# Two graph layers on one core: due times of their own for the first two batches, and head outputs transposed over 97 rows

## The chip, the core and the metric

The kernel runs on one core of one Trainium2 chip. The core has five engines with instruction queues of their own: TensorE (PE; its weight loads are shown apart as PEld), VectorE (DVE), ScalarE (ACT), GpSimd (POOL) and SyncE (SP), which only starts transfers here. Each engine works through its queue in order; engines wait for one another through semaphores. The metric is the time of one execution on the device in microseconds (us); lower is better.

## The reference

Two layers run on `x` of shape (16, 1024, 256), with a 0/1 adjacency matrix `adj` of shape (16, 1024, 1024) of type int32.

```python
# layer 0: attention with 8 heads of 32 columns, masked by adj
e = einsum('whqd,whkd->whqk', q, k)            # q, k, v = heads(x @ Wq), ...
e = where(e >= 0, e, 0.2 * e)
attn = softmax(where(adj > 0, e, NEG), axis=-1)
h = einsum('whqk,whkd->whqd', attn, v)         # -> (w, n, 256)
out = layernorm(h) ; out = concat([out, x]) @ Wffn.T
x1 = layernorm(out) + x
# layer 1: two graph attentions, a norm, a feed-forward, a norm
h = gat(gat(x1, adj, W1, a1), adj, W2, a2)     # softmax of leaky(Wh1 + Wh2^T), masked, axis=1; @ Wh
h = layernorm(x1 + h)
y = layernorm(h + relu(h @ w_ff1 + b_ff1) @ w_ff2 + b_ff2)
```

Each of the 16 batches is independent of the others.

## The kernel before

Everything runs on one core, batch after batch, but the stages of neighbouring batches overlap. A stage is a Python generator, a thread. It yields requests: `take` and `give` for buffers of a pool, `wait` and `fire` for events, `on(PE=..., DVE=...)` for an engine with an estimated cost, and `start` for another thread with an **aim**, a due time. The class `Order` (L34) runs all threads against a plan clock while the kernel is built and emits their instructions. Among the operations that could start within 300 ns of the earliest one, it emits the one with the smallest aim (L150 and what follows). So an aim is a rank: it decides the order on each engine's queue and the order in which waiting threads get buffers, but no engine waits for an aim to pass, except that the scores of a batch may not be planned more than `lead` ahead of theirs (L570). The order is fixed when the program is built; on the chip only semaphores act.

The aims are shares of `SLOT` = 253 us of plan time. They stand in the dictionary `AIM` (L254 to 258). Those of the projections of batch b (`project`, L513) count from the planned start of batch b - 1's scores (`begin`); for batch 0 they count from -253 us. Those of a batch's later stages (`rest`, L968) count from the moment when its last head is planned.

The stages of a batch are these.

- `project`: `x_pair` (L430) loads and transposes x; `qk_part` (L446) makes q and k, splits them in two parts and stores them to DRAM; `load_stacks` (L523) reads them back on SP, head by head; `v_part` (L483) makes v; `make_mask` (L419) starts eight `mask_part` threads (sixteen half ones for batch 0), each of which loads adjacency rows on ACT's queue (L393), turns them to fp8 on DVE (L399), transposes them on PE (L409) and copies them to the mask on ACT (L413). There are two masks; the one of batch b + 2 can be begun when batch b has given its own back, which is after its second graph attention.
- `all_scores` (L558) and `weights` (L585): for each of 8 heads and 8 tiles of 128 keys, scores on PE (L578), scaling on ACT (L596) or, in batch 0, on DVE too (L594), a maximum on DVE (L598), an exponential on ACT (L601) and the product with the mask on POOL (L605). Their aims advance with `pace(b)` (L555): a slot of 253 us, times `fast0` for batch 0 and `fast1` for batch 1. There are five buffers `p` for these tiles.
- `all_values` (L608): the product of the weights with v on PE (L627). v carries a column of minus ones, so 33 columns per head hold the output and its sum. The two halves of the 1024 queries stand one below the other in PSUM, at partitions 0 to 32 and 64 to 96.
- `after_head` (L637): the head's output is copied to SBUF (`ho`), transposed by four PE transposes (L653), and divided by its sums on DVE (L658, L660).
- `rest`: `rows_pair` (L702, layer 0's norms and output), the first graph attention (`attention`, L825, with `attend` on DVE at L814, L817, L820 and the scaling on ACT at L822), `second_rows` (its product, L851), the second graph attention, `normed_pair` (its product, L876), and `feed_forward` (L930; L916 and L944 on PE).

Of the kernel before, what the change touches and what calls it, by code (L numbers as in the profile page):

```python
# [20 lines left out]
P = 128  # L21
# [164 lines left out]
def wait(event):  # L186
    return "wait", event
# [6 lines left out]
def take(pool):  # L194
    return "take", pool
# [6 lines left out]
def start(thread, aim):  # L202
    return "start", (thread, aim)
# [21 lines left out]
def unshifted_path(  # L225
# [8 lines left out]
    nc = tc.nc  # L234
    B, N, D = x.shape
# [15 lines left out]
    PACE = SLOT / (H * NT // 2)  # L251


    AIM = dict(mask0=0.6, x=0.818, x_step=0, mask=0.747, mask_step=0.0264, qk0=0.614, qk1=0.898, qk_step=0.0231, v0=0.832,  # L254
               v1=0.974, v_step=0.0591, rows=-0.244, rows_step=0.0408, first0=0.12, first1=0.252,
               graph0=-0.009, graph1=0.21, graph_step=0, second=0.355, second_step=0.0335, normed=0.78,
               normed_step=0.026, ff_wait=(None, 0, 1, 0), ff=(0.532, -0.011, 0.487, 0.497), ff_step=0.0386,
               fast0=0.4, fast1=0.85, fast15=0.832, lead=3.15)

    const = ctx.enter_context(tc.tile_pool(name="const", bufs=1))  # L260
    sb = ctx.enter_context(tc.tile_pool(name="sb", bufs=1))
# [3 lines left out]
    bufs = dict(misc=3, scores=2, acc=1, p=5, stacks=2, stage=2, adj=2, adjb=2, pair=18,  # L265
                xT=2, v=2, mask=2, hn=1, w8=2, big=1, job=1)
    work = Order(**bufs)

    def misc(dtype=FT):
        return psum.tile([P, HALF], dtype, tag="misc", name="ps_m", bufs=bufs["misc"])  # L270
# [148 lines left out]
    def make_mask(b, t0):  # L419
        yield take("mask")  # L420
        masks[b] = buf([P, NT * N], "mask", "mask", F8)
        parts = [(t, (kh,)) for kh in range(NH) for t in range(NT)] if b == 0 else [(t, (0, 1)) for t in range(NT)]
        for n, (t, halves) in enumerate(parts):
            yield start(mask_part(b, t, halves), t0 + (AIM["mask" if b else "mask0"] + AIM["mask_step"] * n) * SLOT)

    def mask_of(b, t):

# [49 lines left out]
    def project_qk(b, g, t0):  # L477
        scratch[b, g] = dram.tile([2, P, 2, N], FT, name="qk_halves")
        for o in range(2):
            for nh in range(NH):  # L480
                yield start(qk_part(b, g, o, nh), t0 + (2 * o + nh) * AIM["qk_step"] * SLOT)

    def v_part(b, g, u):  # L483
        yield wait(("xT", b, u))
# [18 lines left out]
    def project_v(b, g, t0):  # L503
        yield take("v")
        v = buf([P, NT, G * VW + 31], "v", "v")
        vs[b, g] = v
        yield on(POOL=500)
        nc.gpsimd.memset(v[:, :, G * VW:], 0.0)
        nc.gpsimd.memset(v[:, :, :G * VW].rearrange("p t (h c) -> p t h c", c=VW)[:, :, :, DH:], -1.0)
        for u in range(NP):  # L510
            yield start(v_part(b, g, u), t0 + AIM["v_step"] * u * SLOT)

    def project(b, t0):  # L513
        yield take("xT")
        xTs[b] = buf([P, DC, N], "xT", "xT")
        for u in range(NP):
            yield start(x_pair(b, u), t0 + (AIM["x"] + AIM["x_step"] * u if b else 0.0) * SLOT)
        yield start(make_mask(b, t0), t0 + (0.5 if b else 0.0) * SLOT)
        for g in range(H // G):
            yield start(project_qk(b, g, t0 + AIM[("qk0", "qk1")[g]] * SLOT), t0)  # L520
            yield start(project_v(b, g, t0 + AIM[("v0", "v1")[g]] * SLOT), t0 + (0.8, 1.0)[g] * SLOT)

    def load_stacks():  # L523

# [112 lines left out]
    def after_head(b, h, acc):  # L637
        if h == 0:
            yield take("hn")
            hn[b] = buf([P, NT, D], "hn", "hn")  # L640
            checks[b] = small.tile([P, NSUM + NSCORE], FT, name="check", bufs=2)
            yield fire(("hn open", b))
        yield wait(("hn open", b))
        yield take("pair")
        ho = buf([P, HALF], "pair", "ho")
        engine = yield evacuate(HALF)
        copy(engine, ho, acc)
        yield give("acc")
        yield take("misc")
        pt = misc()  # L650
        yield on(PE=450)
        for i in range(TPH):
            nc.tensor.transpose(pt[:, i * P:(i + 1) * P], ho[:, i * P:(i + 1) * P], ident)  # L653
        yield give("pair")
        src = pt.rearrange("p (i j c) -> p j i c", i=TPH, j=NH)
        rd = checks[b][:, h * NT:(h + 1) * NT].rearrange("p (j i) -> p j i", j=NH)
        yield on(DVE=210)
        nc.vector.reciprocal(rd, src[:, :, :, DH])  # L658
        yield on(DVE=430)
        nc.vector.tensor_tensor(hn[b].rearrange("p (j i) d -> p j i d", j=NH)[:, :, :, h * DH:(h + 1) * DH],  # L660
                                src[:, :, :, :DH], rd[:, :, :, None].to_broadcast([P, NH, TPH, DH]), op=OP.mult)
        yield give("misc")
        yield fire(("hn", b, h))
# [161 lines left out]
    def attention(b, s, rows, at):  # L825

        yield take("w8")
        firsts[b, s] = buf([P, 2, N], "w8", "first")
        for nh in range(NH):
            yield start(first_half(b, s, nh), at(AIM[("first0", "first1")[s]]))  # L830
        for t in range(NT):
            yield wait(("row", b, s, t))
        second = small.tile([P, NT], FT, name="second", bufs=2)
        yield on(ACT=220)
        nc.scalar.activation(second, scores_of(b, s)[:, :, 1], AF.Exp, scale=1.0 - ALPHA)
        sums = small.tile([P, NT], FT, name="sums", bufs=2)
        yield take("big")
        big = buf([P, NT, N], "big", "att")
        yield fire(("graph", b, s))
        for j in range(NT):  # L840
            yield start(attend(b, s, big, rows, j, second, sums), at(AIM[("graph0", "graph1")[s]] + AIM["graph_step"] * j))
        for j in range(NT):
            yield wait(("att", b, s, j))
        yield give("w8")
        return big
# [19 lines left out]
    def normed_pair(b, u, big, y2):  # L865

        tiles = (2 * u, 2 * u + 1)
        yield wait(("x1", b, u))
        x1 = x1s.pop((b, u))
        yield take("misc")  # L870
        pa = misc()
        for i, t in enumerate(tiles):
            for half in range(2):
                yield on(PE=1720)
                for j in range(half * NT // 2, (half + 1) * NT // 2):
                    nc.tensor.matmul(pa[:, i * D:(i + 1) * D], big[:, j, t * P:(t + 1) * P], y2[:, j, :D],  # L876
                                     start=(j == 0), stop=False)
            yield on(PE=430)
            as_rows(pa, i, x1, i)
        yield fire(("weighed", b, u))  # L880
        yield give("pair")
        y, rows, srcs = yield from taken_out(pa, "y")
        mv, rs = yield from stats(srcs)
        yield from normalized(rows, srcs, mv, rs)
        yield take("pair")
        rT = buf([P, DC, 2 * P], "pair", "rT")
        yield take("misc")
        pt = misc()
        yield on(PE=450)
        transposes(pt, rows)  # L890
        yield give("pair")
        for dc in range(DC):
            yield from by_columns(rT[:, dc, :], pt[:, dc * 2 * P:(dc + 1) * 2 * P], k["gl1c"][:, dc:dc + 1],
                                  k["bl1c"][:, dc:dc + 1])
        yield give("misc")

        if b + 1 < B and AIM["ff_wait"][u] is not None:
            yield wait(("graph", b + 1, AIM["ff_wait"][u]))
        yield start(feed_forward(b, u, rT), work.now + (AIM["ff"][u] if b + 1 < B else 0.04 * u) * SLOT)

    def as_rows(pa, i, srcT, t):

# [25 lines left out]
        yield fire(done + (hp,))  # L928

    def feed_forward(b, u, rT):  # L930
        due = work.now + (AIM["ff"][u] if b + 1 < B else 0.04 * u) * SLOT
        yield take("job")
        hid = {}
        for hp in range(HC // 2):
            yield start(hidden(hid, rT, hp, ("hid", b, u)), due + AIM["ff_step"] * hp * SLOT)
        for hp in range(HC // 2):
            yield wait(("hid", b, u, hp))
        yield take("misc")
# [29 lines left out]
    def rest(b):  # L968
# [3 lines left out]
        def at(share):  # L972
            return t0 + share * SLOT
# [6 lines left out]
        for q in range(NH):  # L980
            yield start(head_stats(b, q), at(0))
        for u in range(NP):
            yield start(rows_pair(b, u), at(AIM["rows"] + AIM["rows_step"] * u))
        for u in range(NP):
            yield wait(("hn used", b, u))
        yield give("hn")
# [2 lines left out]
        yield take("w8")  # L989
        y2 = buf([P, NT, YW], "w8", "y2")  # L990
        for i in range(NT):
            yield start(second_rows(b, big, y1, y2, i), at(AIM["second"] + AIM["second_step"] * i))
        for i in range(NT):
            yield wait(("row", b, 1, i))
        yield give("big")
        yield give("w8")
        for u in range(2):
            yield start(fetch_x1(b, u), at(AIM["normed"]))
        big = yield from attention(b, 1, y2, at)
        yield give("mask")  # L1000
        yield start(count(b), at(1.0))
        for u in range(NP):
            yield start(normed_pair(b, u, big, y2), at(AIM["normed"] + AIM["normed_step"] * u))
        for u in range(NP):
            yield wait(("weighed", b, u))
            if u + 2 < NP:
                yield start(fetch_x1(b, u + 2), at(AIM["normed"]))
        yield give("big")
        yield give("w8")

# [409 lines left out]
```

## Time and profile before

| | |
|---|---|
| median of 3 runs | 4531.88 us (4531.49 to 4532.59) |
| the profiled execution | time 4533.91 us, span 4532.1 us, granted clock 0.985 |
| PE busy | 4352.1 us (96%), 20299 matmuls |
| DVE busy | 3338.5 us (74%) |
| ACT busy | 2888.7 us (64%) |
| POOL busy | 2469.0 us (54%) |
| L653, the transposes of the heads' outputs | 512 of 128x128, 80.1 us |
| L605, POOL's product with the mask | 1024, 2228.3 us |

The span runs from the first instruction to the last. An engine's busy time is the time in which at least one of its instructions ran. Ends of matmuls are modelled and their runs overlap, so the distance between starts says more about PE than the length of one. A line such as L653 is a line of the kernel. "Idle before" is the time for which an engine had nothing to do, and behind it stands what ended it.

### The profile page before, as it was taken

The page shows a single profiled execution, that of the slowest core. Times are in us where ns is not written, and L with a number is a line of the kernel's source. Part 1 is how long each engine was busy: PE and PEld are TensorE (multiplying, and loading weights), DVE is VectorE, ACT ScalarE, POOL GpSimd, SP SyncE. Part 2 cuts the span into 40 slices and gives each one's busy share as a digit, 9 for nine tenths or more (in the row PEclk, how much of TensorE's full clock was granted, in tenths as well). Part 3 has the DMA queues.
Part 4 walks back from the last instruction along what each step waited for, and adds up shares of the span by engine and source line. Part 5 has one row for each costly group of instructions (what it writes and reads, how often), then busy time and mean ns, then how long its engine had stood idle before and what let it go on. Part 6 is the DMA issues. An engine that isn't in the chain of part 4 may idle for free.

```text
span 4532.1 us, 57096 instructions
## 1 busy us (share of the span) xinstructions
PE 4352.1 (96%) x20299; PEld 2889.7 (64%) x20299; DVE 3338.5 (74%) x5265; ACT 2888.7 (64%) x4012; POOL 2469.0 (54%) x1544
## 2 busy tenths in 40 slices
PE   7888999999999999999999999999999999999998
PEld 3354756666666676666767666676666667666587
DVE  6876678877787777768777777787768777776754
ACT  5656565566666666676666666666666676666631
POOL 4856465455565545655565565556655564565610
PEclk8989999999999999999999999999999999999999
DMA  6422223132232312323132232322323232232100
GB/s 181 116 65 68 73 61 96 54 84 76 62 98 63 105 56 76 94 59 110 57 88 73 59 100 70 101 66 72 85 66 100 63 93 62 69 92 54 26 22 20
DMA packets 156208, 343.57 MB, mean 76 GB/s; under 512 B 21750, under 2 KB 24332, under 8 KB 155916
## 3 DMA queue, kind: packets, MB, share of 16 engines
q1 hardware_dynamic: 109836, 255.93, 20.2%
q10 hardware_dynamic: 46080, 83.91, 6.2%
q8 instruction: 164, 2.69, 0.3%
q14 instruction: 128, 1.05, 0.1%
HBM read 239.09 MB, written 100.66 MB: 75 GB/s over the span
## 4 chain that ended last, share of the span: by engine, by line
PE 68%; DVE 19%; POOL 5%; issue 4%; ACT 3%; DMA 0%; SPq 0%; ACTq 0%; POOLq 0%; DVEq 0%
PE ps_a L627 15%; PE ps_s L578 9%; PE ps_m L876 8%; PE ps_m L851 7%; PE ps_m L916 7%; PE ps_m L944 6%; DVE att L817 5%; DVE att L814 5%; POOL p L605 4%; DVE p L598 4%; PE ps_m L461 3%; PE ps_m L761 2%; PE ps_m L729 2%; PE ps_m L732 2%; PE ps_m L347 2%
## 5 line engine op out<-in xcount | busy, mean ns | idle before, releaser
L605 POOL TENSOR_TENSOR p<-p,mask 128x1024 f32<-128x1024 f32 x1024 | 2228.3, 2193 | 1588.5 <-ACT p L601 1492.6
L598 DVE TENSOR_TENSOR p<-p,ps_s 128x1024 f32<-128x1024 f32 x1024 | 1210.8, 1213 | 407.9 <-ACT p L596 406.4
L601 ACT ACTIVATE p<-p 128x1024 f32<-128x1024 f32 x1024 | 1081.4, 1058 | 385.8 <-DVE p L598 363.3
L596 ACT ACTIVATE p<-ps_s 128x1024 f32<-128x1024 f32 x996 | 976.6, 1024 | 202.8 <-PE ps_s L578 185.7
L627 PE MATMUL ps_a<-p,v 128*33 128x512 f32 (+1 forms) x4096 | 999.1, 605 | 28.6 <-POOL p L605 27.6
L578 PE MATMUL ps_s<-qs,ks 128*128 128x512 f32 x2048 | 640.4, 432 | 54.5 <-DVE p L598 51.3
L578 PEld LDWEIGHTS ps_s<-qs,ks 128*128 128x128 f32 x2048 | 353.7, 192 | 358.2 <-DVE p L598 118.3
L627 PEld LDWEIGHTS ps_a<-p,v 128*33 128x33 f32 (+1 forms) x4096 | 198.5, 113 | 532.5 <-issue 399.7
L876 PE MATMUL ps_m<-y,att 128*128 128x256 f32 x2048 | 484.3, 383 | 13.7 <-ACT v L499 11.0
L944 PE MATMUL ps_m<-wf,hid 128*128 128x256 f32 x2048 | 478.0, 383 | 9.1 <-ACT xT L305 8.7
L851 PE MATMUL ps_m<-y,att 128*128 128x258 f32 x2048 | 474.4, 382 | 5.6 <-ACT hid L925 3.7
L916 PE MATMUL ps_m<-rT,wf 128*128 128x256 f32 x2048 | 473.6, 380 | 4.2 <-DVE hid L922 1.4
L944 PEld LDWEIGHTS ps_m<-wf,hid 128*128 128x128 f32 x2048 | 382.3, 191 | 77.8 <-issue 14.0
L851 PEld LDWEIGHTS ps_m<-y,att 128*128 128x128 f32 x2048 | 386.7, 190 | 70.4 <-ACT hid L925 4.4
L876 PEld LDWEIGHTS ps_m<-y,att 128*128 128x128 f32 x2048 | 378.8, 191 | 80.1 <-ACT v L499 13.1
L916 PEld LDWEIGHTS ps_m<-rT,wf 128*128 128x128 f32 x2048 | 377.3, 190 | 54.9 <-PE ps_m L461 1.7
L814 DVE SCALAR_TENSOR_TENSOR att<-first,second 128x1024 f32<-128x1024 f32 x256 | 354.0, 1383 | 73.1 <-ACT first L801 73.1
L817 DVE SCALAR_TENSOR_TENSOR att<-mask,att 128x1024 f32<-128x1024 fp8e4 x256 | 363.3, 1419 | 8.7
L822 ACT ACTIVATE y<-y,check 128x258 f32<-128x258 f32 x256 | 130.8, 511 | 321.7 <-DVE check L820 297.9
L330 POOL TENSOR_SCALAR rs<-mv 128x2 f32<-128x2 f32 (+1 forms) x224 | 59.0, 264 | 443.7 <-DVE mv L327 443.6
L399 DVE TENSOR_SCALAR adj_b<-adj_i 128x512 fp8e4<-128x512 int32 x256 | 244.3, 997 | 25.5 <-DMA adj_i<-in_adj_dram 19.3
L925 ACT ACTIVATE hid<-ps_m,columns 128x256 f32<-128x256 f32 x373 | 159.5, 471 | 118.5 <-PE ps_m L916 92.8
(103 smaller groups left out, 4266.9 us busy)
## 6 DMA issues: line engine op xcount, KB each, us to landing
adj_i<-in_adj_dram ACTq DMA_DIRECT2D x256, 256.0 KB, 3.5
qs<-qk_halves SPq DMA_DIRECT2D x256, 256.0 KB, 4.0
ks<-qk_halves SPq DMA_DIRECT2D x256, 256.0 KB, 4.9
qk_halves<-high SPq DMA_DIRECT2D x128, 256.0 KB, 2.5
qk_halves<-low SPq DMA_DIRECT2D x128, 256.0 KB, 3.8
xr<-in_x_dram ACTq DMA_DIRECT2D x64, 256.0 KB, 2.9
x_kept<-x SPq DMA_DIRECT2D x64, 256.0 KB, 2.0
x<-x_kept SPq DMA_DIRECT2D x64, 256.0 KB, 5.3
```

Of the source, the lines that this page charges most:

```text
L578: nc.tensor.matmul(ps[i][:, cols], kk[:, (t + i) * P:(t + i + 1) * P], q[:, cols], start=True, stop=True)
L596: nc.scalar.activation(p, ps, AF.Copy, scale=ALPHA)
L598: nc.vector.tensor_tensor(p, p, ps, op=OP.max)
L601: nc.scalar.activation(p, p, AF.Exp)
L605: nc.gpsimd.tensor_tensor(p, p, mask_of(b, t), op=OP.mult)
L627: nc.tensor.matmul(acc[nh * 64:nh * 64 + m, :], v[:, t, c:c + m], p[:, nh * HALF:(nh + 1) * HALF], start=(t == 0), stop=(t == NT - 1))
L814: nc.vector.scalar_tensor_tensor(e, first[:, 0, :], second[:, j:j + 1], first[:, 1, :], op0=OP.mult, op1=OP.max)
L817: nc.vector.scalar_tensor_tensor(e, mask_of(b, j), -1.0, e, op0=OP.mult, op1=OP.mult, accum_out=sums[:, j:j + 1])
L851: nc.tensor.matmul(pa[:, cols:cols + width], big[:, j, i * P:(i + 1) * P], rows[:, j, :width], start=(j == 0), stop=(j == NT - 1))
L876: nc.tensor.matmul(pa[:, i * D:(i + 1) * D], big[:, j, t * P:(t + 1) * P], y2[:, j, :D], start=(j == 0), stop=False)
L916: nc.tensor.matmul(pa[:, i * 2 * P:(i + 1) * 2 * P], wf1[:, dc, hc * P:(hc + 1) * P], rT[:, dc, :], start=(dc == 0), stop=(dc == DC - 1))
L944: nc.tensor.matmul(pa[:, i * D:(i + 1) * D], hid[hc // 2][:, hc % 2, i * P:(i + 1) * P], wf2[:, hc, :], start=(hc == 0), stop=False)
```

## The change

The kernel gets a second dictionary, `EARLY`, and a function that picks from it for batches below 2. `rest(b)` asks for batch b, the projections of batch b ask for b - 1. So the projections of batches 0, 1 and 2 and the later stages of batches 0 and 1 have aims of their own. In `AIM` itself `mask0`, `fast0` and `fast1` change. In `after_head` the four transposes read the first 64 + 33 = 97 rows of `ho` and write 97 columns each, in the places where they wrote 128. What is read from them afterwards, columns 0 to 32 and 64 to 96, is the same.

```diff
-    AIM = dict(mask0=0.6, x=0.818, x_step=0, mask=0.747, mask_step=0.0264, qk0=0.614, qk1=0.898, qk_step=0.0231, v0=0.832,
-               v1=0.974, v_step=0.0591, rows=-0.244, rows_step=0.0408, first0=0.12, first1=0.252,
-               graph0=-0.009, graph1=0.21, graph_step=0, second=0.355, second_step=0.0335, normed=0.78,
-               normed_step=0.026, ff_wait=(None, 0, 1, 0), ff=(0.532, -0.011, 0.487, 0.497), ff_step=0.0386,
-               fast0=0.4, fast1=0.85, fast15=0.832, lead=3.15)
+    AIM = dict(mask0=0.759, x=0.818, x_step=0, mask=0.747, mask_step=0.0264, qk0=0.614, qk1=0.898,
+               qk_step=0.0231, v0=0.832, v1=0.974, v_step=0.0591, rows=-0.244, rows_step=0.0408, first0=0.12,
+               first1=0.252, graph0=-0.009, graph1=0.21, graph_step=0, second=0.355, second_step=0.0335,
+               normed=0.78, normed_step=0.026, ff_wait=(None, 0, 1, 0), ff=(0.532, -0.011, 0.487, 0.497),
+               ff_step=0.0386, fast0=0.425, fast1=0.938, fast15=0.832, lead=3.15)
+
+    EARLY = dict(x=0.87, x_step=0.005, mask=0.747, mask_step=0.0296, qk0=0.692, qk1=0.909, qk_step=0.0345,
+                 v0=0.774, v1=1.001, v_step=0.0568, rows=-0.139, rows_step=0.0071, first0=0.082, first1=-0.169,
+                 graph0=-0.195, graph1=-0.027, graph_step=0, second=0.302, second_step=0.0335, normed=0.781,
+                 normed_step=0.02, ff_wait=(None, 0, 1, 0), ff=(0.633, -0.001, 0.488, 0.497), ff_step=0.0386)
...
+    def share(b, name):
+        return (EARLY if b < 2 else AIM)[name]
...
-            yield start(mask_part(b, t, halves), t0 + (AIM["mask" if b else "mask0"] + AIM["mask_step"] * n) * SLOT)
+            yield start(mask_part(b, t, halves),
+                        t0 + ((share(b - 1, "mask") if b else AIM["mask0"]) + share(b - 1, "mask_step") * n) * SLOT)
...
+        used = 64 + VW
...
-            nc.tensor.transpose(pt[:, i * P:(i + 1) * P], ho[:, i * P:(i + 1) * P], ident)
+            nc.tensor.transpose(pt[:, i * P:i * P + used], ho[:used, i * P:(i + 1) * P], ident[:used, :used])
...
```

Everywhere else `AIM[...]` becomes `share(b, ...)` in the later stages (`attention`, `normed_pair`, `feed_forward`, `rest`) and `share(b - 1, ...)` in the projections (`project`, `project_qk`, `project_v`).

## The prediction

> **What bounds the kernel now.** I read the page first: its slices, then the chain that ended last. Of the slices, PE, DVE and the granted clock:
>
> ```profile
> PE   7888999999999999999999999999999999999998
> ...
> DVE  6876678877787777768777777787768777776754
> ...
> PEclk8989999999999999999999999999999999999999
> ...
> PE 68%; DVE 19%; POOL 5%; issue 4%; ACT 3%; DMA 0%; SPq 0%; ACTq 0%; POOLq 0%; DVEq 0%
> ```
>
> PE is nearly full from the fourth slice on (a slice is 113 us). Before that it is not, and its clock is not all granted. So TensorE binds, except in the first three batches. Next I cut the span where each batch's last value product (L627) ends, at 221, 481, 795, 1073, 1344 us, and asked for busy times between (columns: window, length, busy us and instructions of PE, PEld, DVE, ACT, POOL, clock, DMA):
>
> ```profile
> 0.00:221.00 221.00, 176.33 (x714) 79.14 (x715) 160.78 (x171) 135.53 (x174) 140.73 (x80) 0.92 0.50 148
> 221.00:481.00 260.00, 224.29 (x932) 130.53 (x931) 187.02 (x264) 159.83 (x208) 156.24 (x85) 0.89 0.26 72
> 481.00:795.00 314.00, 291.31 (x1344) 193.84 (x1342) 229.17 (x349) 186.48 (x258) 167.29 (x96) 0.97 0.26 74
> 795.00:1073.00 278.00, 268.74 (x1272) 178.35 (x1268) 214.28 (x335) 180.43 (x247) 153.03 (x97) 1.00 0.27 76
> 1073.00:1344.00 271.00, 267.25 (x1267) 178.53 (x1266) 204.34 (x325) 182.70 (x254) 152.92 (x97) 1.00 0.27 78
> ```
>
> From the fifth row on every batch takes 271 us with PE 98.6% busy: the regular slot. Batch 2's slot is 314 us, 43 more, and PE's idle time is 45, 36 and 23 us in the first three. Those 104 us, and what the lower clock costs in them, are all that a new order at the front can reach. The third question was what stretches batch 2. The timelines of POOL and ACT answer it (start, length, instruction):
>
> ```profile
> 474.88 2.13 POOL L605 TENSOR_TENSOR p<-p,mask 128x1024 f32<-128x1024 f32 x1 [1.12 <-ACT p L601]
> ...
> 532.79 8.52 POOL L605 TENSOR_TENSOR p<-p,mask 128x1024 f32<-128x1024 f32 x4
> ```
>
> ```profile
> 444.46 0.51 ACT L822 ACTIVATE y<-y,check 128x258 f32<-128x258 f32 x1 [3.47 <-DVE check L820]
> ...
> 448.36 0.82 ACTq L393 DMA_DIRECT2D adj_i<-in_adj_dram  x2
> ...
> 530.41 1.08 ACT L413 COPY mask<-ps_m 128x512 bf16<-128x512 bf16 x2
> ```
>
> Between the last masked product of batch 1 and the first of batch 2 POOL does none for 532.8 - 477.0 = 56 us; in a regular slot that pause is 1.7 us (1070.9 to 1072.6). The product needs batch 2's mask, whose last parts are copied at 531.5. The mask's first load is issued at 448.4, right after the last attention step of batch 0 (L822, 444.5), which frees one of two mask buffers. Those 86 us are as long in a regular slot (1250 to 1336), but there they start 94 us before the slot's end, here 36.
>
> **What the Trainium skill says.** "TensorE: Matmul & The Clock Gate", Back-to-back issue gap: a warm matmul costs its moving columns over 2.4 GHz plus about 2.5 ns. The trace agrees for bf16: two mask transposes of 128 columns take 0.12 us from 25.77 to the next start at 25.89. An fp32 transpose takes about twice that, which the rows below price. The same page, LDWEIGHTS: a load costs by its columns, not by its rows. The trace agrees: 134 ns for 22 rows, 142 on average for 128. The same page, Part 1: a PE idle for a window of about 3.4 us falls to half its clock. It fits 0.92, 0.89 and 0.97 in the first slots against 1.00. "GPSIMD Engine Reference", Specifications: POOL shares its SBUF interfaces with VectorE. The attention step L817 takes 3.03 us while POOL multiplies (median of batch 0), and 1.22 in slot 4.
>
> **The change, part by part.**
>
> *Transposes (L653).* 8 heads x 16 batches x 4 = 512 transposes keep their 128 stationary columns (with 97 rows) and stream 97 identity columns, not 128. The price per column, by starts, since ends are modelled:
>
> ```profile
> 492.48 0.60 PE L653 MATMUL ps_m<-ident,ho 128*128 128x128 f32 x4
> 492.91 0.38 PE L904 MATMUL ps_m<-ident,x 128*128 128x128 f32 x2
> ...
> 1105.17 1.03 PE L732 MATMUL ps_m<-wffnT,hT 128*128 128x256 f32 x4
> 1106.03 1.04 PE L761 MATMUL ps_m<-w,x 128*128 128x260 f32 x4
> ```
>
> Four transposes advance PE by 0.43 us, 108 each; four 256-column passes by 0.86, 215 each. So 107 ns per 128 columns, 0.84 a column, and 31 columns are 26 ns. Sum: 512 x 26 = 13.3 us. In the 13 regular slots and ends where PE is full, 13 x 32 x 26 = 10.8 us; I count that alone, as the first three slots have PE idle. The load is no bound if 97 rows load as 22 do. No row shows 97 columns: at best -13.3, at worst no gain, or +1.5 us if the loads set the pace as in the L1096 row's 112 ns starts (512 x 3). The planner is still told 450 ns, so this part alone moves no instruction. Nobody waits longer: reader L658 starts 0.1 us earlier.
>
> *Aims.* No instruction, wait, buffer or DMA is added; their order on the engines changes. In plan time (253 us to 1.0), with t0 a batch's first scores:
> - Batch 1's scores come due over 237 us, not 215 (0.938 for 0.85); batch 0's over 107, not 101.
> - Batch 2's mask is aimed at 189 to 241; before it was 189 to 236. Relative to the end of batch 1's scores the last part moves from 21 us behind to 4. Its eight parts (16 adjacency loads on ACT's queue, 16 casts, 32 transposes, 8 copies) thus pass the last heads. The first v projections move from 210 to 196.
> - After batch 0's heads, the second product (L851) moves 14 us earlier (0.355 to 0.302) while the scores beside it come due later.
> - The attention aims (0.252 to -0.169 and so on) change little: at 280 and at 398 us they were already due before the scores they compete with.
> - Feed-forward of batches 0 and 1 moves 25 us back (0.532 to 0.633).
>
> Price of the hand-over. Now 8 rows of the second product take 319 to 381 us. By the dues, 2.5 score tiles fall between two rows now; after, about the first 2 rows run at once and 2.3 tiles fall between the rest. A tile costs PE about 1.4 us (two score passes of 0.23, four value passes totalling 0.92), so 20 tiles are 28 us before and 14 are 20 after. Stretched as 62 us stand to the 28 and the 28 of the rows themselves, that is 9; with the two rows run at once I take 12. Batch 0's attention then ends at about 433, and with parts in front of the scores I estimate 60 us for the mask, not 86: ready at 493. Batch 1's softmax ends later, having lost its precedence: 477 becomes 482. The pause shrinks from 56 to about 11 us, by 45. It is not all time, as PE worked in it on batch 0's rest: most of that pause shows PE full, and this work must be done later. What comes back is the starvation of 580 to 740. Slot 2 can't fall below 271, so the bound is 43; half of it, 22, is my estimate. The longer slot 1 costs 5. Net -17, with both ends at -43 and +22 (slot 1 stretched by the whole 237 - 215 and no gain).
>
> *The start.* Batch 0's mask moves from plan -101...-1 to -61...+51, behind its first q and k projections (-98...-80 becomes -78...-52). The mask transposes among the first projections cost PE about 1.5 us; scores wait for the stored q and k to land at 43.8. Against it, the mask's second half was ready at 43.0 and is first used near 57: 14 us of cover. If the cover goes, POOL waits. -2, between -5 and +10.
>
> *Other queues.* SP's and POOL's orders follow from the same dues. Batch 1's projections and their stores on SP are done by about 198 us, before batch 0's last product, so I cost their new order at nothing: POOL goes from batch 0 to batch 1 at 218.5 with 0.3 us between, and if that cover is gone it shows there.
>
> **Sum.** -11 - 17 - 2 = -30. The profiled execution has span 4532.1 and time 4533.9; the median of the runs is 4531.9, within 0.05% of both. 4532 - 30 = 4502 us.
>
> **Rivals.**
> 1. *Only the transposes pay*: the pause closes, but PE does the same work later and nothing is won. For it: PE is busy 19 to 20 of 20 us in most windows of 480 to 560. Against it: 580 to 740 starves with DVE full. 4532 - 11 = 4521.
> 2. *More comes back*: the pause closes, the lower clock goes too, and slot 1 shortens. For it: 104 us of idle. Against it: batch 0 has little other work for PE and POOL is at 141 of 221 us. -11 - 50 = 4471.
> 3. *Slower: slot 1 stretches.* Batch 1's scores yield to batch 0's rest by 237 - 215 = 22 us, but attention, which waits for DVE behind POOL (3.03 us a step), ends as late as now, so the mask is as late and the pause stays. 4532 + 22 - 11 = 4543, and with the deferred feed-forward leaving PE bare in the pause (about 10 us of it ran there) 4553. It decides if attention of batch 0 ends after 445 us and slot 1 after 490.
> 4. *Nothing*: 97 columns cost as much as 128, order neutral: 4532.
>
> **Numbers.** Forecast (4490 to 4512) 0.42; rival 1 (4512 to 4523) 0.18; rival 2 (4450 to 4490) 0.14; rival 4 (4523 to 4541) 0.07; rival 3 (4541 to 4570) 0.19. 0.2% is 9 us, about what a measurement tells from no change. Faster: 0.42 + 0.14 + 0.17 of rival 1 = 0.73; slower 0.19; same 0.08. Leaving out a tenth at each end cuts rival 2 near 4462 and rival 3 near 4556. The forecast's own range is 4490 to 4512.
>
> **What would show it.** L653 starts 83 ns apart; regular slots 0.8 us shorter (270). Last L822 of batch 0 before 440, last L413 of batch 2 before 500, pause of L605 under 25 us, slot 2 under 300. Wrong if the pause stays over 40, if L605 waits for masks near 57 us, or if regular slots grow.

## The result, and the profile after

The changed kernel takes 4492.02 us (median of 4 runs, 4489.66 to 4494.55), the kernel before 4531.72 beside it: a ratio of 0.9912 (95% interval 0.9895 to 0.9929), or 39.7 us less. The profiled execution has time 4494.55 us and span 4492.7 us; its granted clock is 0.990, where it was 0.985.

The page first: PE and its clock in the 40 slices, and the shares of the chain that ended last.

```profile
PE   7888999999999999999999999999999999999998
...
PEclk9989999999999999999999999999999999999999
...
PE 68%; DVE 17%; POOL 5%; issue 5%; ACT 2%; POOLq 0%; ACTq 0%; DVEq 0%
```

At this grain almost nothing differs: one digit of the clock, and 17% for DVE where it was 19%. The page can't place 40 us in 4500; a cut by batches can. I cut again where each batch's last value product ends, L636 in this kernel (columns as in the prediction: window, length, busy us and instructions of PE, PEld, DVE, ACT, POOL, clock, DMA share, GB/s):

```profile
0.00:209.00 209.00, 169.54 (x715) 76.02 (x715) 157.42 (x170) 132.54 (x175) 139.15 (x79) 0.96 0.55 161
209.00:486.00 277.00, 244.85 (x1062) 146.51 (x1063) 198.74 (x290) 171.39 (x227) 163.44 (x90) 0.91 0.25 72
486.00:767.00 281.00, 265.41 (x1236) 174.08 (x1234) 206.05 (x326) 175.97 (x241) 164.81 (x95) 0.98 0.27 75
767.00:1039.00 272.00, 263.97 (x1248) 174.19 (x1246) 208.50 (x330) 179.80 (x248) 152.41 (x97) 1.00 0.27 78
1039.00:1310.00 271.00, 267.21 (x1270) 178.41 (x1267) 204.95 (x326) 183.16 (x254) 153.68 (x97) 1.00 0.28 78
```

With the ends taken to a tenth of a microsecond, in us:

| slot | before | after | difference |
|---|---|---|---|
| 0 | 220.5 | 208.9 | -11.6 |
| 1 | 260.0 | 276.8 | +16.8 |
| 2 | 314.9 | 281.6 | -33.3 |
| 3 | 277.9 | 272.2 | -5.7 |
| 4 to 14, mean of one | 270.6 | 270.1 | -0.5, eleven times: -5.4 |
| 15, and what follows it | 482.0 | 481.6 | -0.4 |

The sum is -39.6 us, the difference of the spans 39.4. Slots 1 and 2 belong together. The third row of the prediction's table held 1344 PE instructions and the second 932; now they hold 1236 and 1062. So slot 1 is longer because it does 130 matmuls more, and slot 2 shorter because it does 108 fewer: work moved from one slot to the other, and the pair is 16.5 us shorter. Over the first four slots, PE's idle time (length less busy) falls from 112 to 95 us, and the clock rises from 0.92, 0.89, 0.97 to 0.96, 0.91, 0.98. So of the 34 us that these four slots lost, 17 are idle time of PE; the other 17 are busy time, with as many matmuls as before (4261 and 4262). Of the busy time, the shorter transposes can account for about 3 (4 slots x 32 x 26 ns). The rest is near what the clock would be worth if busy time grew as the clock falls: on 176, 224 and 291 us of the first three slots about 7, 5 and 3 us, an estimate.

The hand-over from batch 1 to batch 2, as the prediction read it. POOL's products with the mask, and the transfers and copies of ACT:

```profile
479.40 4.23 POOL L614 TENSOR_TENSOR p<-p,mask 128x1024 f32<-128x1024 f32 x2 [3.26 <-PE ps_m L417]
...
495.48 2.13 POOL L614 TENSOR_TENSOR p<-p,mask 128x1024 f32<-128x1024 f32 x1 [2.19 <-ACT mask L421]
```

```profile
422.16 0.51 ACT L832 ACTIVATE y<-y,check 128x258 f32<-128x258 f32 x1 [2.51 <-DVE check L830]
422.41 0.34 ACTq L401 DMA_DIRECT2D adj_i<-in_adj_dram  x1
...
494.82 0.58 ACT L421 COPY mask<-ps_m 128x512 bf16<-128x512 bf16 x1 [1.79 <-PE ps_m L417]
```

Batch 0's attention ends at 422.7 (L832) and the mask's first load follows at once. The last mask copy ends at 495.4, 73 us later, and the first product of batch 2 starts at 495.48, released by that copy. From the last product of batch 1, 483.6, the pause is 11.8 us; it was 55.8.

The transposes, first as two neighbours on PE, then as a group:

```profile
486.62 0.50 PE L663 MATMUL ps_m<-ident,ho 97*128 97x97 f32 x4
486.95 3.04 PE L499 MATMUL ps_m<-wv,xT 128*128 128x128 f32 x24
```

```profile
L663 PE MATMUL ps_m<-ident,ho 97*128 97x97 f32 x512 | 67.4, 254 | 14.7 <-ACT ho L313 8.1 <-DVE ho L311 4.5 <-DVE rT L372 1.2
L663 PEld LDWEIGHTS ps_m<-ident,ho 97*128 97x128 f32 x512 | 54.0, 143 | 57.6 <-issue 16.8 <-ACT ho L313 14.9 <-ACT p L610 10.4
```

Four transposes advance PE by 0.33 us, 83 ns each, where it was 108. The loads take 143 ns on average; with 128 rows they took 142.

### The profile page after: what moved, and what is told of

Same layout as the page of the kernel before. It is cut to its first block, busy times and chain, and to the rows that moved or that the text cites. A ratio compares the mean times of both kernels' runs of the same rounds, so it can differ in the third digit from the quotient of the medians.

```text
span 4492.7 us, 57101 instructions
## 1 busy us (share of the span) xinstructions
PE 4326.9 (96%) x20299; PEld 2871.2 (64%) x20299; DVE 3315.8 (74%) x5262; ACT 2886.4 (64%) x4015; POOL 2472.5 (55%) x1544
## 4 chain that ended last, share of the span: by engine, by line
PE 68%; DVE 17%; POOL 5%; issue 5%; ACT 2%; POOLq 0%; ACTq 0%; DVEq 0%
PE ps_a L636 15%; PE ps_s L587 9%; PE ps_m L887 8%; PE ps_m L862 8%; PE ps_m L927 7%; PE ps_m L955 6%; DVE att L827 5%; DVE att L824 5%; POOL p L614 4%; DVE p L607 3%; PE ps_m L771 3%; PE ps_m L739 2%; PE ps_m L742 2%; PE ps_m L355 2%; PE ps_m L470 2%
## 5 line engine op out<-in xcount | busy, mean ns | idle before, releaser
L636 PE MATMUL ps_a<-p,v 128*33 128x512 f32 (+1 forms) x4096 | 999.3, 606 | 28.9 <-POOL p L614 27.3
L636 PEld LDWEIGHTS ps_a<-p,v 128*33 128x33 f32 (+1 forms) x4096 | 199.6, 114 | 534.5 <-issue 401.1
L955 PE MATMUL ps_m<-wf,hid 128*128 128x256 f32 x2048 | 478.3, 383 | 10.6 <-ACT xT L313 8.9
L955 PEld LDWEIGHTS ps_m<-wf,hid 128*128 128x128 f32 x2048 | 381.8, 191 | 79.1 <-issue 14.8
L887 PEld LDWEIGHTS ps_m<-y,att 128*128 128x128 f32 x2048 | 375.4, 189 | 77.1 <-ACT v L508 13.1
L832 ACT ACTIVATE y<-y,check 128x258 f32<-128x258 f32 x256 | 130.9, 511 | 312.4 <-DVE check L830 292.9
L407 DVE TENSOR_SCALAR adj_b<-adj_i 128x512 fp8e4<-128x512 int32 x256 | 229.8, 940 | 22.0 <-DMA adj_i<-in_adj_dram 12.2
```

Source lines behind the costliest of these rows:

```text
L636: nc.tensor.matmul(acc[nh * 64:nh * 64 + m, :], v[:, t, c:c + m], p[:, nh * HALF:(nh + 1) * HALF], start=(t == 0), stop=(t == NT - 1))
L955: nc.tensor.matmul(pa[:, i * D:(i + 1) * D], hid[hc // 2][:, hc % 2, i * P:(i + 1) * P], wf2[:, hc, :], start=(hc == 0), stop=False)
```

## The experiments

The rival explanations are these. **A**: the three parts (transposes, hand-over, start) pay independently, near the sizes of the prediction. **B**: the aims work only as a set, and a part alone does something else. Later, when two kernels with part of the aims turned out far slower, two more: **C**, their regular slots are long because DVE's attention collides with POOL's product; **D**, they are long because of the order on the engines, which never settles.

Medians in us, with the ratio to the kernel before run beside it; slots as above; "pause" is that of POOL between batches 1 and 2. "Repeats" says whether PE's sequence of lines in one slot equals that of the next from batch 4 to 14; it is read from the instructions of each trace.

| kernel | median | ratio (95%) | slots 0, 1, 2, 3 | mean of 4 to 14 | pause | repeats |
|---|---|---|---|---|---|---|
| before | 4531.72 | | 220.5, 260.0, 314.9, 277.9 | 270.6 | 55.8 | yes |
| after | 4492.02 | 0.9912 (0.9895 to 0.9929) | 208.9, 276.8, 281.6, 272.2 | 270.1 | 11.8 | yes |
| e1_transposes | 4518.31 | 0.9968 (0.9957 to 0.9979) | 220.9, 250.3, 314.5, 277.5 | 270.1 | 55.6 | yes |
| e2_aims | 4500.38 | 0.9932 (0.9919 to 0.9946) | 208.6, 277.1, 280.4, 272.6 | 270.7 | 12.0 | yes |
| e3_start | 4521.47 | 0.9977 (0.9969 to 0.9985) | 206.2, 256.7, 315.5, 277.8 | 270.7 | 56.2 | yes |
| e6_no_start | 4513.03 | 0.9959 (0.9946 to 0.9973) | 219.2, 276.4, 280.1, 272.5 | 270.7 | 11.9 | yes |
| e7_twice | 4524.77 | 0.9988 (0.9980 to 0.9997) | 210.0, 278.0, 283.0, 273.8 | 272.2 | 12.2 | yes |
| e4_fast1 | 4682.09 | 1.0333 (1.0319 to 1.0347) | 220.4, 268.9, 283.7, 274.9 | 286.7 | 10.7 | no |
| e5_fast1_old | 4704.70 | 1.0386 (1.0370 to 1.0401) | 211.8, 264.7, 305.6, 283.6 | 287.0 | 41.5 | no |
| e9_start_fast0_old | 4768.22 | 1.0518 (1.0500 to 1.0535) | 211.0, 270.4, 304.6, 284.7 | 291.1 | 13.9 | no, but every third |
| e12_third_mask | 4839.84, one run | | 222.3, 263.7, 303.2, 294.2 | 296.2 | 22.3 | no |

### The parts

**The transposes alone**, in the kernel before:

```diff
-            nc.tensor.transpose(pt[:, i * P:(i + 1) * P], ho[:, i * P:(i + 1) * P], ident)
+            nc.tensor.transpose(pt[:, i * P:i * P + used], ho[:used, i * P:(i + 1) * P], ident[:used, :used])
```

> The kernel before with the 97-row transposes alone; the order of all instructions stays. Forecast of the prediction: starts 83 ns apart for 109, every regular slot shorter by 32 x 26 = 0.8 us (270.6 becomes 269.8), 4532 - 11 = 4521. Rival: PE's saved time is lost in waits that end when they did (the changed kernel's regular slots are only 0.5 us shorter), 16 x 0.5 = 8 us or less: 4524 to 4528. If the aims carry everything: 4532.

**The aims alone**: the changed kernel with that line as it was.

```diff
-            nc.tensor.transpose(pt[:, i * P:i * P + used], ho[:used, i * P:(i + 1) * P], ident[:used, :used])
+            nc.tensor.transpose(pt[:, i * P:(i + 1) * P], ho[:, i * P:(i + 1) * P], ident)
```

> The changed kernel with its transposes back at 128 rows: the aims alone. If the parts add up, 4492 + 8 to 11 = 4500 to 4503, with slots of 209, 277, 282 us for the first three batches and 270.6 for a regular one. If the shorter transposes also do work in the new order (by closing a wait), more than 4506.

The transposes alone take 13.1 us off, with an interval from 9.5 to 19.5; on top of the aims they take 8.4 off (4500.38 to 4492.02). The aims alone take off 0.68%, 31 us. In e1 the regular slot falls by 0.5 us, and its slot 1 is 250 us against 260. Is that second gain the transposes'? A second profile of the unchanged kernel answers:

> The kernel before once more, to see how far the length of single slots repeats. With the transposes alone, batch 1's slot was 250 us for 260. If that is the transposes' doing, this run shows 260 again, within 2 us; if it is variation from one execution to the next, 250 to 258.

There slot 1 takes 255.6 us with nothing changed (one time, 4530.13 us). So single executions of one kernel differ by some us in that slot, and the 10 us can't be credited to the transposes. The mean of slots 4 to 14 is the better measure: 270.62 and 270.58 us in the two profiles, though single ones range from 270.3 to 271.6. Sixteen slots of 0.5 us are 8, as the rival had it, while e1's median is nearer to the forecast's 4521; where its other 5 us come from stays open.

To see what an added microsecond of PE work costs, the changed kernel with each head's four transposes done twice:

```diff
-        for i in range(TPH):
+        for i in (*range(TPH), *range(TPH)):
```

> The changed kernel with each of the four transposes of a head done twice, to the same place: 512 more transposes of 97 columns, 2.7 us of PE in every batch. If PE's time is the slot's time, regular slots go from 270.1 to 272.8 and the kernel to 4492 + 42 = 4534. If PE's gaps take up half of such work, as the 0.5 us for 0.8 that the shorter transposes brought would say: 271.5 and 4515.

The 512 more transposes of 83 ns are 42.5 us of PE work; the time grows by 32.8 us, 0.77 of it. The ratios' intervals leave some 26 to 43 us for that growth, so the regular slots say more. By starts, the distance from each matmul to the next summed by line (medians of slots 5 to 13), a regular slot gives 2.67 us more to the transposes and gets 2.0 us longer; the scores' line gives up 0.6. In the change itself, the transposes' line falls from 3.49 to 2.73 us in a regular slot, the scores' line rises from 34.32 to 34.52, and the slot falls by 0.47. So part of PE's work here, added or removed, is exchanged with PE's wait at the scores.

**The start alone**: in the kernel before, only the aims of the projections of batch 0, `mask0` and `fast0`.

```diff
-    mask0=0.6, ... fast0=0.4
+    mask0=0.759, ... fast0=0.425
+    def share(b, name):
+        return (EARLY if b < 0 else AIM)[name]
```

> The kernel before with the new aims only at the start: mask0, fast0 and the projections of batch 0. The changed kernel's first slot is 11.6 us shorter. Theory: this comes from these aims and is kept to the end, as PE has less idle time: about 4520. Rival: the time won in batch 0 is lost again in front of batch 2's mask, whose buffer comes free only after the attention of batch 0, so the pause of the masked products grows from 56 us: 4528 to 4532. A third: the shorter first slot comes from the order of batch 1's projections, which this kernel doesn't have: 4530 or more and a first slot of 220.

Its first two slots:

```profile
0.00:206.00 206.00, 167.39 (x713) 76.00 (x713) 157.05 (x170) 132.12 (x174) 139.17 (x78) 0.96 0.57 164
206.00:463.00 257.00, 222.81 (x932) 128.28 (x931) 185.82 (x261) 161.78 (x213) 159.08 (x85) 0.90 0.25 69
```

Slot 0 is 14 us shorter with as many matmuls (713, and 714 before), the later slots stay, and 10 us of it (0.23%) are kept at the end. The scores begin at 44 to 45 us in all three kernels, so the gain isn't an earlier start. Between 60 and 200 us PE waits for DVE's maximum in 8.3 us at the scores' line, where it waited 14.8, and POOL waits for ACT's exponential in 12.0 us, where it waited 17.1 (15.1 and 14.9 us in the second profile of the kernel before). Which of the moved instructions brings that about was not tested.

**All but the start**: the new aims for the rest, with `mask0`, `fast0` and batch 0's projections as they were and transposes over 128 rows.

```diff
-    mask0=0.759, ... fast0=0.425
+    mask0=0.6, ... fast0=0.4
-        return (EARLY if b < 2 else AIM)[name]
+        return (EARLY if 0 <= b < 2 else AIM)[name]
```

> The new aims without those of the start (mask0, fast0 and the projections of batch 0 as before); transposes over 128 rows. Its order repeats from batch 4. If start and hand-over are separate gains: 4532 - (31 - 10) = 4511, first slot 220, pause of the masked products near 12 us. If the hand-over gains only because the start came first: 4525 or more. If the start gains nothing by itself in the new order: 4500.

It takes 0.41% off, 17 to 19 us, with slots 1 to 3 of the changed kernel. Start (-10) and hand-over (-17 to -19) add up to -27 to -29; together they were measured at -31. As far as these four kernels go, the parts of theory A are independent; in size the start is not near its -2.

### The risk that no rival named

**`fast1` alone**: of the whole change only the slower pace of batch 1's scores.

```diff
-               fast0=0.4, fast1=0.85, fast15=0.832, lead=3.15)
+               fast0=0.4, fast1=0.938, fast15=0.832, lead=3.15)
```

> The kernel before with fast1 = 0.938 alone: batch 1's scores due over 237 us for 215. Theory: everything else passes them (second product, mask, v), the pause falls from 56 us to about 25 and the time to about 4520. Rival (the prediction's slower case): batch 1's slot stretches from 260 to 270 or more while the attention of batch 0 ends no earlier than 445 us, the pause stays over 45 us: 4540.

Its hand-over is that of the changed kernel: the pause is 10.7 us, and the first three slots sum to 773 us, against 795 before and 767 after. Yet the time is 150 us longer. The loss is in slots that should be regular; slots 3 to 7:

```profile
773.00:1048.00 275.00, 264.39 (x1231) 172.19 (x1232) 202.38 (x325) 179.52 (x249) 151.96 (x97) 0.99 0.27 77
1048.00:1333.00 285.00, 273.09 (x1276) 181.48 (x1275) 207.13 (x334) 182.69 (x251) 154.63 (x97) 0.99 0.26 74
1333.00:1618.00 285.00, 269.22 (x1267) 180.24 (x1265) 209.30 (x343) 175.28 (x234) 150.90 (x96) 0.98 0.26 74
1618.00:1915.00 297.00, 276.30 (x1270) 182.36 (x1271) 214.68 (x338) 178.72 (x241) 154.90 (x97) 0.98 0.25 71
1915.00:2212.00 297.00, 278.73 (x1295) 186.02 (x1294) 224.72 (x333) 179.33 (x246) 164.08 (x96) 0.98 0.26 71
```

PE is idle for 11 to 21 us of each of these, where a settled slot has 4, and the slots differ from one another. The reverse, **all new aims with `fast1` as it was** (and transposes over 128 rows):

```diff
-               fast0=0.425, fast1=0.938, fast15=0.832, lead=3.15)
+               fast0=0.425, fast1=0.85, fast15=0.832, lead=3.15)
```

> All the new aims but fast1, which stays 0.85; transposes over 128 rows. In this program PE's order of work in one batch never repeats in the next (in the kernel before and in the changed one it repeats exactly from batch 4 on; in the run with fast1 alone it does not). Theory: what counts is that the plan of the first batches ends in the repeating order; without it the regular slots are 275 to 300 us for 271 and the attention step of DVE meets POOL's products (over 2 us for 1.22): over 4600. Rival: aims act where they stand; without fast1 batch 2's mask is late again and the pause of 56 us comes back: 4515 to 4525.

It is 175 us slower than the kernel before beside it, with a pause of 41.5 us and regular slots of 287 us. And **e3 with `fast0` as it was**:

```diff
-               fast0=0.425, fast1=0.85, fast15=0.832, lead=3.15)
+               fast0=0.4, fast1=0.85, fast15=0.832, lead=3.15)
```

> The kernel with the new aims of the start alone, but with fast0 back at 0.4: one number differs from the run that took 4521. In its program PE's order never repeats from one batch to the next. If the repeating order is what the time hangs on: over 4600, regular slots of 275 to 300 us, attention steps of over 2 us. If fast0 acts only on batch 0: within 10 us of 4521.

One number, 0.4 for 0.425, makes 4768 of 4521 us. Its slot 0 is 211 us, so most of the start's gain is there; against e3, 224 of the 251 us by which the span grew are lost in slots 4 to 14. So theory A does not hold for every subset of the aims, and B is right of these three.

What the slow kernels have in common is in the last column of the table. In the fast ones, the sequence of lines on PE in a slot equals that of the slot after it, ten times in a row from batch 4 on (a similarity of 1.00, counted as twice the common lines over all lines). In e4, e5 and e9 it never does: 0.50 to 0.74. The orders are fixed when the program is built, so this can be read from it before it runs.

But an order that differs from slot to slot may still settle, and in e9 it does. From slot 6 on, each slot has the order of the third one after it (0.99 to 1.00), and the three that alternate stay long. Slots 9 to 11, and 12, which begins the cycle anew:

```profile
2521.00:2820.00 299.00, 278.87 (x1301) 187.65 (x1299) 220.30 (x335) 181.97 (x250) 163.66 (x97) 0.98 0.24 71
2820.00:3109.00 289.00, 269.24 (x1246) 177.97 (x1245) 218.81 (x335) 177.76 (x242) 161.56 (x98) 0.98 0.25 73
3109.00:3395.00 286.00, 267.81 (x1253) 176.68 (x1252) 206.78 (x337) 177.74 (x241) 152.59 (x96) 0.98 0.26 74
3395.00:3693.00 298.00, 279.36 (x1298) 188.79 (x1298) 218.22 (x335) 181.70 (x250) 164.62 (x97) 0.97 0.24 71
```

So "never settles", as D has it, is not what makes a slot long. What the fast kernels share is one certain cycle: with lines matched across the edits, the settled slot is the same in the kernel before, the changed one, e1, e2, e3 and e6 (1.00). e4 shows the other side. In slot 14 it has come to exactly that order (1.00), and that slot takes 270.7 us, where none of slots 4 to 13 took less than 275. The aims of the first two batches are used up by slot 4; what they leave behind can only be the planner's state: its clocks, its buffers and waiting threads. That is an argument, not a measurement.

**Does C explain it?** In e4, between 1600 and 2200 us, the attention step L817 by form:

```profile
L817 DVE SCALAR_TENSOR_TENSOR att<-mask,att 128x1024 f32<-128x1024 fp8e4 x32 | 70.8, 2212 | 1.1
```

In the kernel before it takes 1225 ns in the same stretch. The mean of 2212 hides two values: 15 of the 32 steps have no product of POOL beside them and take 1.22 to 1.23 us, 17 have one and take 3.03 to 3.21. To shorten POOL's part, its product was halved in both:

```diff
-        nc.gpsimd.tensor_tensor(p, p, mask_of(b, t), op=OP.mult)
+        nc.gpsimd.tensor_tensor(p[:, :HALF], p[:, :HALF], mask_of(b, t)[:, :HALF], op=OP.mult)
```

These two kernels leave out the masking of half the queries. The sums that come out of it make the kernel run its second, general path afterwards, which is some 13 ms of their times; only the slots are to be read.

> The kernel with fast1 = 0.938 alone, and POOL multiplies only the first 512 of the 1024 columns of each tile with the mask; the other half of the masking is left out. Same order as the run that took 4682. If its slots of 275 to 303 us come from DVE's attention steps meeting POOL's products, this falls to 270 to 274 and the kernel towards 4540. If the order itself makes PE wait: slots of 280 or more stay, the kernel over 4620.

> The kernel before with the same half of the masking left out: what the shorter POOL product is worth in the repeating order. PE sets the regular slot there, so 268 to 271 us for 270.6, and a gain of 0 to 50 us in the first three slots, where POOL and DVE set the pace: 4480 to 4530.

In e4 with the half product the step takes

```profile
L817 DVE SCALAR_TENSOR_TENSOR att<-mask,att 128x1024 f32<-128x1024 fp8e4 x34 | 57.8, 1701 | 1.2
```

and ten of its slots (1000.9 to 3780.9 us) average 278.0 us, against 288.3 with the whole product; in the kernel before with the half product a regular slot takes 267.4 us. The excess over the kernel before falls from 288.3 - 270.6 = 17.7 to 10.6 us, by 40%; neither expectation was met as written. Nor does this alone decide, since the step's loss was halved and not removed: 2212 - 1225 = 987 ns became 476 (18 of the 34 steps lie beside a halved product and take 2.06 to 2.24 us). (The Trainium skill, "GPSIMD Engine Reference", Specifications, says that POOL shares its SBUF interfaces with VectorE; that the step is long only beside POOL's products, and less so beside half ones, agrees.) The single slots of e4 decide it better. In slots 4, 5, 9, 10, 12 and 13 L817 takes 1225 ns on average, as in a settled slot, and still they take 285.2, 284.9, 275.3, 285.2, 290.3 and 275.8 us: 12.2 too many on average. In slots 6, 7, 8 and 11, where it takes 1.9 to 2.5 us, the excess is 26. So of the 177 us that these ten slots have too much, C can explain the difference of the two, 4 x 14 = 56, about a third, if those four would else have the excess of the six. The rest is there without it.

What happens in slot 5 (1333 to 1618 us) is seen in one stretch of 19 us, busy times first, then PE, DVE and POOL:

```profile
1504.00:1523.00 19.00, 6.88 (x20) 3.75 (x20) 18.48 (x31) 6.06 (x13) 0.00 (x0) 0.80 0.04 14
```

```profile
1509.56 1.98 PE L461 MATMUL ps_m<-xT,wk 128*128 128x512 f32 x4 [1.58 <-ACT hid L925]
1522.03 1.22 PE L944 MATMUL ps_m<-wf,hid 128*128 128x256 f32 x2 [10.49 <-DVE hn L660]
```

```profile
1499.90 1.52 DVE L814 SCALAR_TENSOR_TENSOR att<-first,second 128x1024 f32<-128x1024 f32 x1
...
1519.98 1.22 DVE L817 SCALAR_TENSOR_TENSOR att<-mask,att 128x1024 f32<-128x1024 fp8e4 x1
...
1521.55 0.42 DVE L660 TENSOR_TENSOR hn<-ps_m,check 128x256 f32<-128x256 f32 x1
```

```profile
1524.33 2.13 POOL L605 TENSOR_TENSOR p<-p,mask 128x1024 f32<-128x1024 f32 x1 [24.00 <-ACT p L601]
```

DVE runs eight attention steps in a row, from 1499.90 to 1521.2. The division of a head's output, L660, stands behind them in DVE's queue, and with it the buffer of PSUM (`ps_m`, one of three) that it reads. PE stands idle for 10.49 us until L660 has given it back, POOL has no product for 24 us, and the clock in the stretch is 0.80. The attention steps L817 here take their 1.22 us, so no collision makes this wait; it comes from the order in DVE's queue. In a settled slot PE's longest idle stretch is 1.0 us.

Over slots 4 to 13, PE is idle for 151 us in e4 and for 37 in the kernel before. Those 114 us are most of the 177; the rest is busy time, 2732 us for 2670, at a clock of 0.98 for 1.00. The largest parts of e4's idle time are 27 us behind L660, 32 behind ACT's `hid` (L925) and 26 behind DVE's maximum (L598), and none of these three ends a wait of PE over 0.15 us in the settled slots. With half the product 21, 22 and 6 us are left: the waits for the maximum go with POOL's product, those behind L660 and `hid` mostly stay. In e9 the ones behind L660 (L670 there) are 74 us, and of its three alternating slots the one of 286 us has no attention step longer than 1.23 us. So D holds in a narrower form. The order of these slots is not that of the one good cycle, whether it settles or not, and it costs queue waits as here and collisions with POOL besides. Why one set of aims leads into that cycle and its neighbour doesn't stays open.

### The gate of the mask

The prediction put the mask's start down to the buffer that batch 0's second attention gives back. A third mask takes that wait away; to fit, the `pair` buffers go from 18 to 15.

```diff
-    bufs = dict(... pair=18, xT=2, v=2, mask=2, ...)
+    bufs = dict(... pair=15, xT=2, v=2, mask=3, ...)
```

> The kernel before with a third mask buffer, paid for with three of the 18 pair buffers. Its order doesn't repeat, so only the first slots are to be read, and the whole will be over 4600. If the freeing of a mask buffer after batch 0's attention holds batch 2's masked products back, its mask is loaded before that attention ends and the pause of 56 us falls under 15. If the mask is late because its aim ranks behind batch 1's scores, the pause stays over 40.

ACT's mask copies beside the last attention step of batch 0, then POOL's products at the hand-over:

```profile
397.77 1.08 ACT L413 COPY mask<-ps_m 128x512 bf16<-128x512 bf16 x2
...
446.75 0.51 ACT L822 ACTIVATE y<-y,check 128x258 f32<-128x258 f32 x1 [2.48 <-DVE check L820]
...
503.34 0.58 ACT L413 COPY mask<-ps_m 128x512 bf16<-128x512 bf16 x1
```

```profile
480.67 4.22 POOL L605 TENSOR_TENSOR p<-p,mask 128x1024 f32<-128x1024 f32 x2 [2.44 <-ACT p L601]
...
507.16 2.14 POOL L605 TENSOR_TENSOR p<-p,mask 128x1024 f32<-128x1024 f32 x1 [1.17 <-ACT p L601]
```

The mask now begins 49 us before that attention ends, and the pause falls from 56 to 22 us: the gate was real. But the pause is not under 15, as was expected of a gate that is all of it. The mask's eight copies are spread over 106 us, to 503.9, so their rank among the other work holds the last of them back too. The order with these buffers is not the good cycle either, so the whole time says nothing on the gate.

## Why the prediction was right, and where not

The forecast was 4502 us, the time is 4492, inside the forecast's own range. Its terms were -11, -17 and -2; measured they are -8 to -13, -17 to -19 and -10.

- **Transposes, -11.** The price of 0.84 ns a column held: 83 ns for 97 columns, and 143 ns for the load, so the loads set no pace. The Trainium skill ("TensorE: Matmul & The Clock Gate", Back-to-back issue gap) gives N / 2.4 + 2.5 ns for the gap of a warm matmul of N columns taken by itself. With N doubled for f32, as the 108 ns before suggest, that gives 2 x 97 / 2.4 + 2.5 = 83 ns and 109 for 128 columns, an estimate, and both agree with the starts. "Regular slots 0.8 us shorter" is the step that was mis-sized: it is 0.5, because PE's wait at the scores takes back 0.2 of the 0.76 us and other lines a little. It was counted as if a PE that is 98.6% busy had nothing to wait for.
- **Hand-over, -17: right in sum, in part by luck, as errors cancel.** "Attention of batch 0 ends at about 433" came out at 423, but 11.6 us of that are the earlier slot 0. From the end of slot 0, attention took 214 us where it took 224.5 (220 in the second profile of the kernel before): 6 to 11 us, where 12 were estimated. Nor do they lie where the estimate had them. All 12 were to come in the second product; it took 56 us for 61, its first two rows start 9 us apart and not at once, and another 6 us lie between its end and the second attention (12 for 18). "60 us for the mask" was 73. "The longer slot 1 costs 5" was 17, with 130 matmuls drawn in from slot 2. "Slot 2 falls by 22" was 33. The pause of 11 us was met at 11.8. What it was worth was a choice of the prediction ("half of it, 22, is my estimate"), not a sum; the pair of slots gave 16.5.
- **Start, -2: mis-sized, -10.** The term weighed only the mask transposes among the first projections and the load of q and k, before 57 us. The gain lies after that, from 60 to 200 us, where PE and POOL wait less in batch 0's scores. The pace `fast0` was listed (107 for 101 us) and not priced; but with the old `fast0` slot 0 is still 9.5 of the 14 us shorter (e9, 211.0), so most comes with the mask and the projections that the term did weigh. The idle time of the first slot, 45 us, was named as within reach, and the term put nothing on it.
- **Other queues at nothing.** POOL passes from batch 0 to batch 1 with 1.2 us between (0.3 before). The cover held, and near 57 us POOL waits for no mask.
- **Rival 1** (nothing won by closing the pause) falls: e2 and e6 win without the transposes. **Rival 3** had its first half right: slot 1 does stretch by 17 us, to 485.7, four us short of its own point of decision; but attention ended before 445, so the pause closed. **Rival 2**'s more came in part, by the start and the clock. Rival 4 falls with e1 and e2.
- **Two small misreadings.** PE reaches nine tenths in the fifth slice, not the fourth, and 0.355 to 0.302 of 253 us is 13 us, not 14. No term rests on either.
- **What the prediction lacked.** It took the regular slots as given, with only "wrong if regular slots grow" as a trace of doubt. Three partial sets of these aims made them grow by 16 to 20 us each, which costs 150 to 240 us, four to six times the gain. That the whole set keeps the order of the regular slots could have been read from the built order alone, and the prediction's chances had no case for it. In that much, too, the forecast was lucky.

## What to carry to other kernels

In a schedule planned once and run through the same stages again and again, look first whether the order on the bounding engine repeats from one iteration to the next, and whether it is still the cycle that was good; an edit at the front can keep that cycle or lose it, and here that outweighed what the edit gained in its own place. That an order repeats is not enough: the cycle of three slots in e9 was 20 us a slot slower. Price a front edit by the sum of neighbouring slots, since work moves from one to the next, and don't read one stretched slot as a loss. Measure small parts in the mean of the steady slots, which agreed to 0.1 us here, and not in a stage whose length varies from run to run.

## What was not expected of the hardware

- Of PE work added to or taken from a slot in which PE is 98.6% busy, about a quarter (e7: 2.67 us added to a slot, 2.0 longer) to two fifths (0.76 us removed, 0.47 shorter) was exchanged with waits.
- One stage of one program can vary between executions by as much as the whole: slot 1 of the kernel before took 260.0 us in one and 255.6 in another, whose times differ by 3.8 us in 4530. The mean of slots 4 to 14 differed by less than 0.1.
- DVE's attention step L817 took 1.22 to 1.23 us with no product of POOL beside it, and 3.03 to 3.21 beside a whole product, 2.06 to 2.24 beside a half one (e4 and its half, 1600 to 2200 us); and no such collision was needed for a slot to be 14 us too long.
